# Step 0's attention over the nodes that a tile keeps, gathered by number, in a loop of small steps

## The chip, the cores and the metric

The kernel runs on one core of one Trainium2 chip. The metric is the time of one execution on the device in microseconds (us). Before the change three runs gave 1848.92, 1849.03 and 1849.40 us; the median is 1849.03. The profile was taken on an execution of its own, of 1845.05 us.

## What is computed

Two layers of a graph network on N = 3327 nodes with 256 features. Layer 0 is graph attention over a sparse adjacency (each row has a handful of neighbours) with a GRU cell and a layer norm; its result is X. Layer 1, which the change concerns, does two steps (n = 0 and 1):

```python
Xf = X
Xa = X
for n in range(STEPS):
    A = _top_p_attention(Xa, W1, W2, W3)
    Xf = R @ Xf
    Xa = A @ Xa
    Z = Z + Xf @ U1[n].T + Xa @ U2[n].T
```

`_top_p_attention` makes q = Xa W1ᵀ W2ᵀ, k = Xa W3ᵀ (64 wide), the logits q kᵀ and their softmax over all nodes. In each row it keeps the most probable nodes, as many as are needed to reach 0.9 of the sum, drops the others and divides by the sum of what is kept. R is the adjacency with the identity added, each row divided by its sum. The output is the layer norm of X + Z, added to X and normalized again.

## The kernel before

The rows are cut into NT = 26 tiles of 128 (the last has 127). Layer 0 (`Layer0.run`) runs its tiles in a software pipeline: `tile` (L835) is a generator whose pieces are numbered steps, a new tile starts every EVERY = 6 phases, and in each phase every open tile does one step, the oldest first. Within `manual_schedule` the instructions of the named engines keep the order in which the program writes them, PE, ACT, DVE and POOL in layer 0. At its end `Shared.qk` (L616) makes a tile's query and key: transposes, two products, copies into `qT` and `kT`. `first_logits` (L1009) already makes most logits of the first two tiles of step 0.

Layer 1 (`Layer1.run`, L1816) is one loop over 52 items, 26 tiles of step 0 and then 26 of step 1; PE, ACT and DVE keep the program's order there, POOL and the DMA queues of SP are ordered by the framework. An item goes through these pieces, spread over three turns of the loop:

- `chunk` (L1194): logits of the tile in eight pieces of 416 nodes, product on PE (L1201), copy out of PSUM on ACT (L1204);
- `list_1` (L1265): `eights` (L1217) takes the eight largest of every 208 nodes on DVE, `sort` (L1235, L1237) the 40 largest of those in order;
- `exp` (L1285) of all logits with the row's sum, `exp_list` of the 40 on ACT;
- `list_3` (L1304) with `settle` (L1240): running sum of the list, the least kept logit, and flags if the list was too short;
- `mask` (L1316): one DVE instruction over all 3327 nodes (L1325) sets what isn't kept to zero and sums the row;
- `product` (L1748): `turn` transposes the masked tile in 26 pieces on PE (L1408) and copies them on ACT (L1410, L1412), `times` (L1424) multiplies them with the 26 pieces of x1 (step 0) or xa (step 1);
- `scaled` (L1435) divides by the sum; in step 0 `rest` (L1742) then makes the next step's query and key, in four pieces between the products of the next item.

Beside it `fetch` (L1348) gathers the neighbours' rows with five indirect DMAs of POOL (L613) and makes five comparisons m on POOL (L1362); `propagate` (L1364) multiplies them (L1370). In step 0 POOL also makes `own` and x1 + bias (L1375 to L1380) and SP stores three arrays per tile.

```python
            slots = [[] for _ in range(7)]
...
                slot(5, self.mask, i + 1)
...
            self.product(i, slots)
```

The slots are the seven groups of `product`: what an item's product doesn't use of DVE and ACT is filled with the sorting, exp and mask of the next item and the logits of the next but one. Where step 0 ends (`new_step`) nothing can be filled in: the last tile's keys must exist before the logits of step 1 are complete.

If a flag in `bad` is set at the end, a slow version of the whole kernel runs after it; with these inputs it doesn't in the kernel before.

## Time and profile before

| what | value |
|---|---|
| profiled execution: its own time / span | 1845.05 / 1843.2 us |
| median of the runs | 1849.03 us |
| busy over the span: PE, DVE, ACT, POOL | 1642.9, 1317.1, 1022.7, 1157.2 us |
| last key copy of layer 0 ends | 390.3 us |
| first and last product of step 0 start | 407.3 and 973.8 us |
| first and last product of step 1 start | 998.9 and 1579.4 us |
| one round of step 0 (800.00 to 821.84): PE, DVE, ACT, POOL busy | 21.55, 12.74, 12.70, 14.20 us |
| mean granted TensorE clock | 0.962 of full |

In the profile a line gives engine, source line, operation, the tile written and those read, partitions x elements and count; then busy time, the mean duration of one and the idle time before it with what ended it. PE is TensorE's products, PEld its weight loads, DVE VectorE, ACT ScalarE, POOL GpSimd, SP the queue that issues most DMAs. In an answer by stretches each line has the stretch, its length, the busy time of each engine with its number of instructions, the granted TensorE clock, the busy share of the DMA engines and GB/s. In a timeline a line has start, duration, engine, line, operation and count, and in brackets the idle time before it.

### The profile page before, as it was taken

Reading aid. Unit: us, or ns where it says so; the run is one execution under the profiler, and the core shown is the slowest. Engines: PE = TensorE matmul, PEld = TensorE weight load, DVE = VectorE, ACT = ScalarE, POOL = GpSimd, SP = SyncE. Lnnn points to the kernel's source line nnn. Section 1 sums busy time; section 2 is a strip of 40 time slices with the busy share of each in tenths; the row PEclk is TensorE's granted clock in tenths of the full one; section 3 lists DMA queues with packets and bytes.
Section 4 is the critical chain, followed back from the end, with each engine's and each line's share of the span. In section 5 each row is a group of like instructions: output and inputs, shape, how many; then the busy total and the mean of one; then the engine's idle time right before and its main releaser. Section 6 shows DMA issues by size and latency. Waiting matters only on the chain. (4 is left out here: it accounts for less than half of the span.)

```text
span 1843.2 us, 27552 instructions
## 1 busy us (share of the span) xinstructions
PE 1642.9 (89%) x8093; PEld 1210.1 (66%) x8093; DVE 1317.1 (71%) x4100; ACT 1022.7 (55%) x2365; POOL 1157.2 (63%) x1902
## 2 busy tenths in 40 slices
PE   7488899969999999999996999999999989788992
PEld 5255555647777777777774777777777656677882
DVE  6788887455555665655546999999999877967751
ACT  3366666646565555555554555555555537558454
POOL 2577777557886666666655556566666583666654
PEclk9799999979999999999998999999999999899996
DMA  9876672222221111111101111111111120213321
GB/s 278 306 242 220 218 218 70 59 63 78 83 58 41 41 41 42 44 48 47 43 24 43 46 47 49 52 52 52 47 49 50 49 62 22 75 56 97 103 87 44
DMA packets 95098, 154.21 MB, mean 84 GB/s; under 512 B 16470, under 2 KB 68173, under 8 KB 94940
## 3 DMA queue, kind: packets, MB, share of 16 engines
q1 hardware_dynamic: 63818, 86.51, 14.4%
q0 software_dynamic: 20384, 53.28, 11.0%
q10 hardware_dynamic: 10738, 12.58, 2.1%
q8 instruction: 66, 1.08, 0.2%
q14 instruction: 92, 0.75, 0.1%
HBM read 124.65 MB, written 27.75 MB: 83 GB/s over the span
## 5 line engine op out<-in xcount | busy, mean ns | idle before, releaser
L1410 ACT COPY at<-pt 128x512 f32<-128x512 f32 (+2 forms) x364 | 191.6, 541 | 261.1 <-PE pt L1408 261.1
L1424 PE MATMUL pav<-xa,at 128*128 128x256 f32 (+2 forms) x1352 | 329.2, 388 | 7.3 <-ACT at L1410 7.3
L1424 PE MATMUL pav<-x,at 128*128 128x256 f32 (+2 forms) x1352 | 325.7, 385 | 7.6 <-ACT at L1410 7.6
L1424 PEld LDWEIGHTS pav<-xa,at 128*128 128x128 f32 (+2 forms) x1352 | 244.6, 190 | 86.5 <-ACT at L1410 41.0
L1424 PEld LDWEIGHTS pav<-x,at 128*128 128x128 f32 (+2 forms) x1352 | 244.4, 190 | 72.4 <-ACT at L1410 29.9
L1204 ACT COPY array<-pl 128x416 f32<-128x416 f32 (+4 forms) x405 | 183.1, 502 | 182.4 <-PE pl L1201 182.3
L1217 DVE MAX8 cand<-array 128x8 f32<-128x167 f32 (+5 forms) x921 | 239.0, 336 | 44.6 <-ACT array L1204 44.6
L613 POOL DMA_INDIRECT g<-xf_rows,edge x130 | 136.5, 1050 | 156.4 <-PE pxf L1370 124.1
L613 POOL DMA_INDIRECT g<-x_rows,edge x130 | 139.9, 1076 | 104.0 <-PE ptq L626 71.2
L1201 PE MATMUL pl<-kT,qT 64*128 64x416 f32 (+4 forms) x810 | 198.0, 560 | 4.5 <-ACT x L1599 2.7
L1309 DVE TENSOR_TENSOR_SCAN before<-e 128x40 f32<-128x40 f32 (+3 forms) x52 | 14.4, 276 | 224.2 <-ACT e L1302 224.2
L1362 POOL TENSOR_SCALAR m<-col,erow 128x128 f32<-128x128 f32 x260 | 162.8, 640 | 14.5 <-PE pxf L1370 8.0
L613 POOL DMA_INDIRECT g<-whx,edge x130 | 141.3, 1087 | 46.3 <-issue 36.1
L1370 PE MATMUL pxf<-g,m 128*128 128x256 f32 (+1 forms) x520 | 133.0, 404 | 14.7 <-POOL m L1362 8.0
L1370 PEld LDWEIGHTS pxf<-g,m 128*128 128x128 f32 (+1 forms) x520 | 98.6, 198 | 69.3 <-issue 41.9
L1235 DVE MAX8 lst<-cand 128x8 f32<-128x160 f32 (+3 forms) x364 | 114.5, 315 | 9.0
L1408 PE MATMUL pt<-ident,array 128*128 128x128 f32 (+1 forms) x676 | 100.9, 276 | 7.0 <-DVE array L1325 7.0
L819 DVE FIND_INDEX8 at<-ones,array 128x8 uint32<-128x840 f32 (+1 forms) x104 | 105.5, 1027 | 0.0
L1408 PE MATMUL pt<-ident,p 128*128 128x128 f32 (+2 forms) x676 | 99.6, 273 | 3.7 <-DVE p L1325 3.7
L1408 PEld LDWEIGHTS pt<-ident,array 128*128 128x128 f32 (+1 forms) x676 | 84.8, 144 | 24.8 <-PE pxf L1370 8.0
L1408 PEld LDWEIGHTS pt<-ident,p 128*128 128x128 f32 (+2 forms) x676 | 83.8, 143 | 20.8 <-PE pxf L1370 7.4
L1325 DVE SCALAR_TENSOR_TENSOR array<-array,t,array 128x3327 f32<-128x3327 f32 x26 | 96.0, 3692 | 0.5
(458 smaller groups left out, 3277.2 us busy)
## 6 DMA issues: line engine op xcount, KB each, us to landing
array<-in_adj_dram SPq DMA_DIRECT2D x23, 1248.0 KB, 6.7
array<-in_adj_dram SPq DMA_DIRECT2D x23, 415.5 KB, 6.4
xf_rows<-xf SPq DMA_DIRECT2D x50, 128.0 KB, 1.8
xa_rows<-xa SPq DMA_DIRECT2D x50, 128.0 KB, 1.7
xfs<-xf_rows SPq DMA_DIRECT2D x50, 128.0 KB, 2.4
whx<-table ACTq DMA_DIRECT2D x25, 129.5 KB, 3.9
x_rows<-x ACTq DMA_DIRECT2D x25, 128.0 KB, 1.7
xb_rows<-xb SPq DMA_DIRECT2D x25, 128.0 KB, 1.8
```

The source lines that it names most:

```text
L613: self.nc.gpsimd.indirect_dma_start(out=dst[:, b, :], out_offset=None, in_=table[:, :], in_offset=bass.IndirectOffsetOnAxis(ap=self.edge[: ...
L819: nc.vector.max_index(at[:r, g, :], self.ones8[:r], ad[:r, g, :])
L1201: nc.tensor.matmul(pl[:r, :w], q[on], self.sh.kT[on, n, s : s + w], start=True, stop=True)
L1204: nc.scalar.copy(l[:r, h * HALF + s : h * HALF + s + w], pl[:r, :w])
L1217: self.nc.vector.max(cand[:r, g * 8 : g * 8 + 8], src[:r, g * group : min(N, (g + 1) * group)])
L1235: nc.vector.max(lst[:r, k : k + 8], cand[:r])
L1325: nc.vector.scalar_tensor_tensor(v.p[:r], v.l[:r, :N], v.t[:r], v.p[:r], ALU.is_ge, ALU.mult, accum_out=sA[:r])
L1362: nc.gpsimd.tensor_scalar(v.m[:, b, :], sh.col1, sh.erow[:, v.at, b : b + 1], None, ALU.is_equal)
L1370: nc.tensor.matmul(acc[:r, :D], v.m[:, b, :r], v.g[:, b, :], start=(b == 0), stop=(b == EB - 1))
L1408: nc.tensor.transpose(pt[: rows(j), j - j0, :r], v.p[:r, cols(j)], self.ident[:r, :r])
L1410: nc.scalar.copy(at[:, :full, :r], pt[:, :full, :r])
L1424: nc.tensor.matmul(v.acc[: v.r, :D], at[:k, j - 4 * g, : v.r], V[:k, j, :], start=(j == 0), stop=(j == NT - 1))
```

## The change

Step 0 leaves the loop and gets one of its own, built like layer 0's: `sparse` is a generator of some 46 steps, a new tile starts every EVERY0 = 8 phases, and PE, ACT, DVE and POOL all keep the program's order. Logits, eights, sort and exp stay. The threshold becomes a limit half way between the least kept and the greatest dropped logit. Then nothing is masked or transposed: signs of logit minus limit (bf16) are made by ACT for the first 17 blocks of nodes and by DVE for the rest, PE counts over the rows which nodes any row of the tile keeps (`pc`), and these are numbered with a running sum (`pp`, `upto`, `at`). A place is split into a low part (32) and a high part (20); from both one-hot arrays are made (`hot`), and their product over all blocks gives the list of nodes by place (`pu`, `node`). The list goes through DRAM (`ulist`) to get one node per partition in five columns, and five indirect DMAs of POOL gather rows of `x1k`: features, a one and the key of step 0, 321 numbers. The logits of the gathered nodes are made once more, transposed (`plt`), with the limit subtracted by a product of ones and a diagonal; exp, and what is under 1 is set to zero. Five products with the gathered rows give the sum of features and, in the 257th column, the row's sum. More than 640 nodes in a tile set a flag in `bad`.

Layer 0's `qk` also makes the key by rows and stores the row of `x1k`, two DMAs on ACT's queue. The comparisons m of the propagation (L1362) are made by DVE in step 0, and the own row comes in by a product with the identity. x1 + bias moves to step 1 (`x_and_bias`), two tiles per item. `u1` is loaded after step 0, into the space of step 0's keys. The first two items' logits and the first one's eights of step 1 are made while the last tiles of step 0 run out (`first_1`). The loop over items now has step 1 alone.

```diff
...
+EVERY0 = 8
+UB = 5
+UL, UH = 32, UB * P // 32
+
+KX = D + 1 + DA
+
+ROUND = 1.5 * 2.0 ** 23
+
+SIGNS = (0, 8 * P, 17 * P)
...
+        if n == 0:
+
+            for c in range(DC):
+                nc.tensor.matmul(
+                    pq[:r, P : P + DA], xt[:, c, :r], self.wkqk[:, c, :DA], start=(c == 0), stop=(c == DC - 1)
+                )
...
+        if n == 0:
+            onek = self.onek[t % 2]
+            nc.scalar.copy(onek[:r, 1:], pq[:r, P : P + DA])
+            move_rows(nc.scalar, self.x1k[t * P : t * P + r, :D], src, r)
+            move_rows(nc.scalar, self.x1k[t * P : t * P + r, D:], onek[:r, :], r)
...
+    def sparse(self, t):
...
+        for k, pair in enumerate(self.chunks()):
+            yield from to(2 * k)
...
+                copies = [self.chunk(0, l, self.q(0, t), r, h, s, tag) for h, s in pair]
...
+            yield from to(2 * k + 1)
+            for copy in copies:
+                copy()
+            yield from to(2 * k + 2)
+            for h, s in pair:
+                c = h * HALF + s
...
+                    self.eights(v.cand, l, r, GROUP[0], c, min(N, c + LC))
+            if k < 3:
+                continue
+            v.last = self.last_eights(v.cand, r, tag)
+            sort = self.sort(v.cand, r, LIST[0], tag)
+            lst = next(sort)
+            nmax = small("nmax0", f"nmax{tag}")
+            nc.vector.tensor_scalar(nmax[:r], lst[:r, 0:1], -1.0, None, ALU.mult)
+        g1 = work.tile([P, EB, D], F32, tag="g", name=f"g{tag}")
+        sh.gather(g1, sh.x1_rows, t, (0, 1))
+        both = self.p[t % 2].bitcast(BF16)
+        signs, hot = both[:, : N + 1], both[:, N + 1 : N + 1 + NT * 2 * (UL + UH)].rearrange("p (b e) -> p b e", b=NT)
...
+        yield from to(9)
+        nc.scalar.activation(signs[:r, :HALF], l[:r, :HALF], AF.Exp, bias=nmax[:r], accum_out=sums[:r, 0:1])
+        next(sort)
+        next(sort)
+        sh.gather(g1, sh.x1_rows, t, (2,))
+        yield from to(10)
...
+        sh.gather(g1, sh.x1_rows, t, (3,))
+        yield from to(11)
+        nc.scalar.activation(e[:r, 1:], lst[:r, : LIST[0] - 1], AF.Exp, bias=nmax[:r])
+        sh.gather(g1, sh.x1_rows, t, (4,))
+        m1 = work.tile([P, EB, P], F32, tag="m", name=f"m{tag}")
+        for b in range(EB):
+            nc.vector.tensor_scalar(m1[:, b, :], sh.col1, sh.erow[:, t, b : b + 1], None, ALU.is_equal)
+        yield from to(12)
+        nc.scalar.activation(signs[:r, HALF:N], l[:r, HALF:N], AF.Exp, bias=nmax[:r], accum_out=sums[:r, 1:2])
+        yield from to(13)
...
+        nc.vector.tensor_tensor_scan(before[:r], e[:r], e[:r], 0.0, ALU.add, ALU.add)
...
+        nc.vector.tensor_scalar(thr2[:r], sums[:r, 0:1], sums[:r, 1:2], 2.0 * TOP_P, ALU.add, ALU.mult)
...
+        nc.vector.tensor_scalar(out[:r], before[:r], thr2[:r], BIG, ALU.is_ge, ALU.mult)
+        nc.vector.tensor_scalar(kept[:r], before[:r], thr2[:r], -BIG, ALU.is_lt, ALU.mult)
+        nc.vector.tensor_tensor(out[:r], out[:r], lst[:r], ALU.add)
+        nc.vector.tensor_tensor(kept[:r], kept[:r], lst[:r], ALU.add)
...
+        nc.vector.tensor_reduce(least[:r], out[:r], AX.X, ALU.min)
+        nc.vector.tensor_reduce(most[:r], kept[:r], AX.X, ALU.max)
+        nc.vector.tensor_scalar(most[:r], most[:r], v.last[:r], lst[:r, LIST[0] - 1 :], ALU.max, ALU.max)
+        nc.vector.tensor_scalar(self.flag[:r, 0, t : t + 1], most[:r], least[:r], None, ALU.is_ge)
+        nc.vector.tensor_scalar(most[:r], most[:r], least[:r], -0.5, ALU.add, ALU.mult)
+        nc.vector.tensor_scalar(least[:r], least[:r], -1.0, 1.0, ALU.mult, ALU.add)
...
+        nc.vector.tensor_tensor(limit[:r], most[:r], least[:r], ALU.min)
+        acc1 = self.pac.tile([P, 512], F32, tag="av", name=f"pxf{tag}")
+        nc.tensor.matmul(acc1[:r, :D], self.ident[:r, :r], sh.x1[:r, t, :], start=True, stop=False)
+        for b in range(EB):
+            nc.tensor.matmul(acc1[:r, :D], m1[:, b, :r], g1[:, b, :], start=False, stop=(b == EB - 1))
+        yield from to(14)
...
+        nc.scalar.activation(xf2[:r], acc1[:r, :D], AF.Copy, scale=sh.rinv[:r, t : t + 1])
+        move_rows(nc.sync, sh.xf_rows[t * P : t * P + r, :], xf2[:r], r)
...
+        nc.vector.memset(signs[:, N:], 0.0)
+        nc.scalar.activation(signs[:r, s0:s1], l[:r, s0:s1], AF.Sign, bias=limit[:r])
+        yield from to(15)
+        nc.scalar.activation(signs[:r, s1:s2], l[:r, s1:s2], AF.Sign, bias=limit[:r])
...
+        nc.vector.tensor_scalar(bound[:r], limit[:r], -1.0, None, ALU.mult)
+        nc.vector.tensor_scalar(signs[:r, s2:N], l[:r, s2:N], bound[:r], None, ALU.is_ge)
+        yield from to(17)
+        pc = self.psm.tile([P, 512], F32, tag="sm", name=f"pc{tag}")
+        for b in range(NT):
+            nc.tensor.matmul(
+                pc[:, b : b + 1], signs[:r, b * P : (b + 1) * P], self.ones16[:r, 0:1], start=True, stop=True
+            )
+        yield from to(18)
...
+        nc.vector.tensor_scalar(any_[:, :full], pc[:, :full], 0.5 - r, None, ALU.is_gt)
+        nc.vector.tensor_scalar(any_[:, full:], pc[:, full:NT], 0.5, None, ALU.is_gt)
+        yield from to(19)
+        pp = self.psm.tile([P, 512], F32, tag="sm", name=f"pp{tag}")
+        nc.tensor.matmul(pp[:, :NT], sh.lower16, any_, start=True, stop=True)
+        nc.tensor.matmul(pp[:, NT : 2 * NT], self.ones16, any_, start=True, stop=True)
+        yield from to(20)
...
+        nc.vector.tensor_tensor_scan(upto, pp[:, NT : 2 * NT], self.zeros, 0.0, ALU.add, ALU.add)
+        nc.gpsimd.tensor_copy(self.needed[:, t : t + 1], upto[:, NT - 1 :])
...
+        nc.vector.tensor_tensor(at, upto, pp[:, NT : 2 * NT], ALU.subtract)
+        nc.vector.tensor_tensor(at, at, pp[:, :NT], ALU.add)
...
+        whole = upto
+        nc.vector.tensor_scalar(whole, at, 1.0 / UL, (1.0 - UL) / (2.0 * UL), ALU.mult, ALU.add)
+        nc.vector.tensor_scalar(whole, whole, ROUND, None, ALU.add)
+        nc.vector.tensor_scalar(whole, whole, -ROUND, None, ALU.add)
+        nc.vector.scalar_tensor_tensor(low, whole, -float(UL), at, ALU.mult, ALU.add)
+        nc.vector.scalar_tensor_tensor(high, any_, -128.0, whole, ALU.mult, ALU.add)
...
+        nc.vector.tensor_tensor(hot[:, :, e0:e1], wide(low, UL), deep(self.places_l, UL), ALU.is_equal)
+        yield from to(21)
+        nc.vector.tensor_tensor(hot[:, :, e1:e2], wide(high, UH), deep(self.places_h, UH), ALU.is_equal)
+        nc.vector.tensor_scalar(hot[:, :, :e0], hot[:, :, e0:e1], self.fromend, None, ALU.mult)
+        nc.vector.tensor_tensor(hot[:, :, e2:e3], hot[:, :, e1:e2], wide(self.block, UH), ALU.mult)
+        yield from to(22)
+        pl = self.psm.tile([P, 512], F32, tag="sm", name=f"pu{tag}")
+        for b in range(NT):
+            nc.tensor.matmul(
+                pl[:e1, : 2 * UH], hot[:, b, :e1], hot[:, b, e1:e3], start=(b == 0), stop=(b == NT - 1)
+            )
+        yield from to(23)
...
+        nc.scalar.activation(node, pl[UL:e1, UH : 2 * UH], AF.Copy, scale=float(P))
+        yield from to(24)
+        nc.vector.tensor_tensor(node, node, pl[:UL, :UH], ALU.add)
+        nc.sync.dma_start(self.ulist[t].rearrange("(l h) -> l h", h=UH), node)
...
+        nc.sync.dma_start(back, self.ulist[t].rearrange("(p b) -> p b", b=UB))
+        yield from to(27)
...
+        nc.gpsimd.tensor_scalar(idx, back, -1.0, float(N + 1), ALU.mult, ALU.add)
...
+        def gather(b):
+            nc.gpsimd.indirect_dma_start(
+                out=g2[:, b, :], out_offset=None, in_=sh.x1k[:, :],
+                in_offset=bass.IndirectOffsetOnAxis(ap=idx[:, b : b + 1], axis=0),
...
+            )
+        gather(0)
+        yield from to(28)
+        gather(1)
+        gather(2)
+        yield from to(29)
+        gather(3)
+        yield from to(30)
+        gather(4)
+        yield from to(33)
+        pt = self.ptr.tile([P, 512], F32, tag="tr", name=f"pk{tag}")
+        for b in range(UB):
+            k, on = g2[:, b, D + 1 :], slice(b // 2 * P, (b // 2 + 1) * P)
+            if b % 2:
+                nc.tensor.matmul(pt[DA:, on], k, self.ident, start=True, stop=True)
+            else:
+                nc.tensor.transpose(pt[:DA, on], k, self.ident)
...
+        nc.scalar.activation(diag[:r, :r], self.ident[:r, :r], AF.Copy, scale=limit[:r])
+        yield from to(34)
...
+        nc.scalar.copy(kg[:, : UB // 2, :], pt[:, : UB // 2 * P].rearrange("p (j c) -> p j c", c=P))
+        nc.scalar.copy(kg[:DA, UB // 2, :], pt[:DA, UB // 2 * P : (UB // 2 + 1) * P])
+        yield from to(35)
+        pls = [self.ptr.tile([P, 4, P], F32, tag="tr", name=f"plt{tag}_{k}") for k in range(2)]
+        for k, n in enumerate(((UB + 1) // 2, UB // 2)):
+            nc.tensor.matmul(
+                pls[k][:, :n, :r], sh.ones[:r, :], diag[:r, :r].unsqueeze(1).to_broadcast([r, n, r]),
+                start=True, stop=False,
+            )
+        for b in range(UB):
+            on = slice(b % 2 * DA, (b % 2 + 1) * DA)
+            nc.tensor.matmul(
+                pls[b % 2][:, b // 2, :r], kg[on, b // 2, :], self.q(0, t)[on], start=False, stop=(b + 2 >= UB)
+            )
+        yield from to(37)
...
+        for k, n in enumerate(((UB + 1) // 2, UB // 2)):
+            nc.scalar.activation(w[:, k::2, :r], pls[k][:, :n, :r], AF.Exp)
+        yield from to(38)
+        nc.vector.scalar_tensor_tensor(w[:, :, :r], w[:, :, :r], 1.0, w[:, :, :r], ALU.is_ge, ALU.mult)
+        yield from to(39)
+        acc = self.pac.tile([P, 512], F32, tag="av", name=f"pav{tag}")
+        for b in range(UB):
+            nc.tensor.matmul(acc[:r, : D + 1], w[:, b, :r], g2[:, b, : D + 1], start=(b == 0), stop=(b == UB - 1))
+        yield from to(40)
...
+        nc.vector.tensor_scalar(rA[:r], acc[:r, D : D + 1], 1e-30, None, ALU.max)
+        nc.vector.reciprocal(rA[:r], rA[:r])
+        yield from to(42)
+        xa = self.xa[:r, t, :]
+        nc.scalar.activation(xa, acc[:r, :D], AF.Copy, scale=rA[:r])
+        move_rows(nc.sync, sh.xa_rows[t * P : t * P + r, :], xa, r)
+        yield from to(43)
+        yield from sh.qk(self.psm, self.work, 1, t, xa)
+    def step_0(self):
+        tiles, first = [], self.first_1()
+        self.done = self.phase = 0
+        while self.phase < EVERY0 * NT or tiles:
+            if self.phase % EVERY0 == 0 and self.phase // EVERY0 < NT:
+                tiles.append(self.sparse(self.phase // EVERY0))
+            for g in list(tiles):
+                if next(g, True):
+                    tiles.remove(g)
+                    self.done += 1
+            next(first, None)
+            self.phase += 1
...
...
+    def first_1(self):
...
+        while self.phase < EVERY0 * NT + 8:
+            yield
...
+        self.fetch(NT)
...
+        for pair in self.chunks():
+            while self.done * P < min(NT * P, HALF + pair[0][1] + LC):
+                yield
+            for i in (NT, NT + 1):
+                self.some_logits(i, pair)
+                yield
...
+    def x_and_bias(self, t):
+
+        nc, sh, r = self.nc, self.sh, rows(t)
+        xb = self.work.tile([P, D], F32, tag="own", name=f"xb{t}", bufs=2)
+        nc.gpsimd.tensor_tensor(xb[:r], sh.x1[:r, t, :], self.b[:r], ALU.add)
+        move_rows(nc.sync, sh.xb_rows[t * P : t * P + r, :], xb[:r], r)
...
+        engines = {mybir.EngineType.PE, mybir.EngineType.Activation, mybir.EngineType.DVE}
+        with self.tc.manual_schedule(engines=engines | {mybir.EngineType.Pool}):
+            self.step_0()
+        with self.tc.manual_schedule(engines=engines):
+            self.list_1(NT)
...
+            self.load_u1()
+            for i in range(NT, total):
...
+                for t in range(2 * (i - NT), 2 * (i - NT) + 2):
+                    if t < NT:
+                        self.x_and_bias(t)
...
```

## The prediction

> **What bounds the kernel now.** I read the busy shares of the page first, then the busy time by stretches, which cuts the span into stages: layer 0 up to about 390 us, step 0 from 407 to 974, step 1 from 999 to 1580, the ends after that.
>
> ```profile
> core 0: us, PE busy (x) PEld busy (x) DVE busy (x) ACT busy (x) POOL busy (x), PEclk, DMA share, GB/s
> 390.00:407.30 17.30, 7.44 (x22) 5.39 (x22) 13.90 (x50) 5.55 (x12) 13.76 (x13) 0.52 0.25 65
> 407.30:974.00 566.70, 557.01 (x2832) 420.60 (x2832) 319.04 (x1073) 323.34 (x688) 387.80 (x451) 1.00 0.17 50
> 974.00:998.90 24.90, 9.37 (x37) 6.46 (x36) 17.99 (x52) 8.03 (x17) 7.47 (x14) 0.69 0.08 19
> 998.90:1579.60 580.70, 550.10 (x2749) 410.29 (x2748) 527.68 (x1613) 315.81 (x612) 351.23 (x596) 0.99 0.18 49
> ```
>
> The reader is to see: in step 0 PE works 557 of 566.7 us, 26 rounds of 21.84 us, one tile each; DVE and ACT have over 40% to spare. So step 0 is bound by PE, with the 26 transposes (L1408) and 26 products (L1424) of a tile. Step 1 is bound by PE and DVE together and isn't rewritten.
>
> Three timelines give the prices that the page's means don't: what an instruction costs inside a queue.
>
> ```profile
> 244.69 0.17 PE L889 MATMUL pe<-tell,mem 128*128 128x20 bf16 x1
> 244.72 0.17 PE L890 MATMUL pe<-tell,mem 128*128 128x19 bf16 x1
> ...
> 825.93 1.99 PE L1424 MATMUL pav<-x,at 128*128 128x256 f32 x8 [0.29 <-ACT at L1410]
> ```
>
> Small bf16 products start 0.025 us apart although each shows 0.17; fp32 ones of 256 columns are two instructions of about 0.217 each.
>
> ```profile
> 837.21 0.24 DVE L1247 TENSOR_SCALAR out<-before,pay 128x40 f32<-128x40 f32 x1
> 837.49 0.20 DVE L1249 SCALAR_TENSOR_TENSOR kept<-out,lst 128x40 f32<-128x40 f32 x1
> ...
> 838.31 3.67 DVE L1325 SCALAR_TENSOR_TENSOR array<-array,t,array 128x3327 f32<-128x3327 f32 x1
> ```
>
> Small DVE instructions that wait for each other stand 0.16 to 0.3 us apart; the mask over all nodes (L1325) is one of 3.67.
>
> ```profile
> 829.52 1.00 POOL L613 DMA_INDIRECT g<-x_rows,edge  x1 [0.30 <-issue]
> 838.48 3.60 POOL L1261 TENSOR_SCALAR many<-d 128x1 f32<-128x1 f32 x1
> ```
>
> A gather occupies POOL for 1.30 us with its gap. The 3.60 us of L1261, on one element per row, are POOL held by DVE's mask.
>
> **What the Trainium skill says.** "SBUF — State Buffer", section "SBUF: two separate sides": DVE and GpSimd share a port pair under an exclusive lock. The trace agrees for POOL (the 3.60 us); it shows no DVE instruction stretched by gathers: the mask of layer 0 (L884) took 535 to 599 ns in all 26 calls while POOL gathered almost without pause. "VectorE: DVE Perf Modes", section "Mode 2×_1P": a two-tensor instruction gets two results a cycle only with 16-bit data at step 1; the new comparisons read one operand at step 0, so I take one element a cycle. L900 (80 elements, 0.243 us) gives the fixed part, about 0.16. "TensorE: Matmul & The Clock Gate", section "Part 1: The HAM clock gate": TensorE falls to half clock after an idle window of some 3.4 us. The trace agrees in kind: 1.00 where PE is full, 0.52 and 0.69 where it is mostly idle.
>
> **The change, part by part.** Worked out in float64 from the reference's inputs, a row of step 0 keeps 1 to 32 nodes and the 128 rows of a tile together 369 to 513. So 640 places suffice everywhere, and the slow path isn't taken for that.
>
> PE, per tile. Gone: 26 transposes × 0.14 = 3.6 and 52 × 0.217 = 11.3. Kept: logits 16 × 0.175 = 2.8, propagation 2.2, query and key 0.8. Added: one identity product 0.4, counts and list 54 bf16 products × 0.025 and their latency 1.7, five key turns 0.9, logits by node 1.75, five products 2.2. Sum 12.8: PE is no longer the bound.
>
> ACT: the copies at/pt (L1410) go, two Signs come (1664 elements took 1.69, so 1.05 and 1.2), with small ones: 14.2.
>
> POOL: ten gathers × 1.30, two small ones: 13.7; the five comparisons m, own, xb, and the held flags leave it.
>
> DVE, per tile: MAX8 16 × 0.281 = 4.5; sorting 3.2 (both as in the timeline of before); five comparisons m at 0.2 from L561's 0.268 = 1.0; threshold 13 small × 0.21 = 2.7; Sign's DVE share 1151 elements: L884 took 0.54 for 640, so 0.8, with bound and memset 1.0; any 0.3; numbering 8 small = 1.85; one-hot: 832 elements / 0.96 + 0.16 less overlap 0.95, 520 elements twice 0.62, one scalar multiply 0.3, sum 2.5; node 0.2; weights 640 elements 0.8; reciprocal 0.4; the rest 0.25. Sum 18.7 against 12.74 now. One-hot at two elements a cycle would make it 17.7; every small one at 0.25 instead makes it 19.7. So **DVE is the new bound**, with 18.7 against today's 21.84.
>
> Waits that stay. Tiles start every eight phases and each engine's order is fixed, so I laid one round out by hand. Two waits don't fit. First, the numbering's prefix product pp stands on PE behind the logits by node, which wait for ACT's key copy kg, itself behind Exp 1.69, two copies 0.88 and two small 0.9 after nmax; PE then needs 1.9, so pp is ready 5.55 us after nmax, and DVE arrives after 4.98 (sort 2.5, any, MAX8, m): 0.6 us, with DVE's whole queue behind it. Second, rA waits for the five products, 2.5 us after the weights, where DVE has 2.1 of other work: 0.45. PE will be about 65% busy; the first 100 us (59%) show a clock of 0.86, the ends (76%) 0.90, the stretch 360 to 407 (66%, with single waits of over 3 us) 0.78. I take 0.88, which lengthens the 3.95 us of PE in these two chains by 0.55. Round: 18.7 + 0.6 + 0.45 + 0.55 = 20.3.
>
> The list's way through DRAM: store landing 1.8, load 2.0 (xf_rows and xf in the page's DMA issues); three phases, about 6 us, lie between: hidden. The new wait is POOL's: `uidx` waits for the list, and behind it stand this tile's five gathers and one of a younger tile; POOL has 6 us of slack a round. If that cover went, the 4 us would fall there, then on PE's key turns. On SP, behind `back`, wait only xa's and xf's stores, not needed soon.
>
> Step 0 as a whole, from the last key copy at 390 to the first product of step 1. Before: 998.9 − 390 = 609 us. After: five opening rounds, by the DVE work of the one to five tiles present (the first is a wait for the last logits): 3 + 13 + 17.5 + 17.8 + 19 = 70; 21 full rounds × 20.3 = 426; one round without new MAX8 17; then the last tile alone: list 9, DRAM 4.5, POOL (which first serves step 1's fetch, 9.5, and the tile before) until 25.4, landing 2, keys to key copy 12.3, logits and MAX8 of step 1's first tile 3.3, its sort, exp and mask 17.2 as now (979.9 to 997.1): 60. Sum 573. Gain 36.
>
> Layer 0: two more products per tile (four instructions × 0.13 = 0.5 us on PE), one copy and two DMA issues on ACT (0.9 us). POOL sets the pace there: it never waits, a round is 11.37 us, ACT waits 2.75 for its `shift` each round, PE is idle about 1.25. Both are covered until the last five tiles, where PE runs without gaps: 5 × 0.5; at the end 1.6 of ACT's issues stand before the first logits. I take 5; without the cover 13 to 23; a gain is excluded, since only work is added.
>
> Step 1: xb's addition (0.73 on POOL) and store move there, two per tile for 13 tiles; POOL is 60% busy, SP far less: 1, at worst 4 through the shared port. The load of u1 moves off the start, unread until the ends: 0.
>
> Sum: −36 + 5 + 1 = −30 on the profiled execution: span 1843.2, so 1813; its own time of 1845.05 becomes 1815. The median of the runs is 1849.03, 4 us above that execution, so **1819**.
>
> **Rivals.**
> (a) The waits close: if the chain to pp beats DVE by its missing 0.6, the reciprocal finds its products ready and the clock stays full, a round is 18.7 and the step saves 34 more: 1785. For: layer 0, built the same way, keeps its bound engine full. Against: my layout of the order.
> (b) Slower, by TensorE's clock. PE's gaps in a round reach 2 to 3 us; if they count as idle, the 3.95 us of PE in the two chains stretch: at 0.6 by 2.63 instead of 0.55, 21 × 2.1 + 4 = 48 us more: 1867. It decides from a clock of about 0.68 down, where the stretch is 1.8 a round in place of 0.55 and eats the 30 us. For: 0.69 at 974 to 999. Against: 0.86 to 0.90 in the stages nearest in load.
> (c) POOL becomes the bound: DVE's two-input and fast-mode instructions fill some 9 us of a round, and each of ten gathers may be held. From 0.8 us a gather POOL passes 21.7; at 1.0 a round is 23.7: 1890. Against: in layer 0, beside a DVE 85% busy, gathers took 1.09 on average against 1.00.
> (d) Layer 0 pays in full and the numbering costs 0.6 more: everything is given back, 1849.
>
> **How the numbers follow.** Forecast 0.45 (its own range 1800 to 1840), (a) 0.25, (b) 0.15, (c) 0.08, (d) 0.07. Below 0.2% (3.7 us) a measurement here can't tell from no change. Faster 0.45 + 0.25 = 0.70; same 0.06 of (d); slower the rest, 0.24. The range leaves out 0.08 below 1775 (rounds under 18.2) and 0.12 above 1868 (most of (c), half of (b)).
>
> **What would show it.** In the changed profile: step 0's DVE near 92% busy and PE near 65%; 26 tiles' xa in rounds of 20.3; DVE waiting 0.5 to 1.2 us for PE at the numbering (pp) and at rA, and for little else; POOL's gathers near 1.0 to 1.1; PEclk 0.85 to 0.9; layer 0's last x_rows store within 5 us of today's; step 1's rounds unchanged at 22.3. I am wrong if DVE waits in more places than these two, if the small instructions stand further apart than 0.21, or if step 1 moves.

## The result, and the profile after

The changed kernel takes 1958.47 us (median of 4 runs, 1954.40 to 1963.17; the kernel before beside it 1848.97). The ratio is 1.0595 with a 95% interval of 1.0569 to 1.0622: slower by 6%, where 1819 was forecast. The profiled execution has a span of 1957.8 us against 1843.2, so 114.6 us are to be found.

The stages of the changed kernel, as busy time by stretches (columns as before: stretch, length, busy time of PE, PEld, DVE, ACT and POOL, granted clock, DMA share, GB/s): twenty rounds of step 0, step 1's first twelve items, its other fourteen.

```profile
478.40:919.40 441.00, 358.98 (x2381) 231.54 (x2381) 333.08 (x1421) 255.65 (x541) 223.98 (x241) 0.88 0.31 80
...
1034.80:1371.50 336.70, 277.44 (x1265) 203.60 (x1264) 249.50 (x761) 139.47 (x275) 208.22 (x296) 0.90 0.16 47
1371.50:1693.30 321.80, 298.94 (x1483) 223.18 (x1484) 282.69 (x853) 176.13 (x338) 195.54 (x321) 0.98 0.17 48
```

The reader is to see two things. In step 0 no engine is full: DVE works 333 of 441 us (76%), PE 359 (81%); a round takes 22.05. So DVE isn't the bound that was forecast; waits are. And step 1, whose code is hardly touched, is slow in its first part: in the 336.7 us of twelve items, eleven take 27.7 to 30.6 each, where an item before took 21.8; afterwards it is back at 21.8 until the items that were longer before the change too.

Between the landmarks of the stages (the start of layer 0's last key copy, step 1's first product, its last product, the end) the time moved like this:

| us | before | after | difference |
|---|---|---|---|
| layer 0, to its last key copy | 390.0 | 399.2 | +9.2 |
| step 0, from there to step 1's first product | 608.9 | 635.6 | +26.7 |
| step 1, to its last product | 580.6 | 658.5 | +77.9 |
| ends | 263.7 | 264.5 | +0.8 |

The waits of the changed kernel, longest first, of which these lines matter (engine, instruction and line, what it waited for: us in total, times, longest us):

```profile
DVE upto L1355 <- PE pp L1352: 77.4, 24, 4.2
PE pos L1823 <- POOL flag L1821: 73.0, 13, 9.2
...
DVE rA L1451 <- PE pav L1448: 43.2, 26, 5.2
...
POOL own L1687 <- DMA xb_rows<-xb: 23.0, 11, 3.2
```

The second and the last belong to step 1. The other two are the two waits that the prediction had named; in the twenty rounds of step 0 they are 65.5 and 23.5 us, 4.45 a round, where 1.6 was forecast.

**Step 1, one slow item.** POOL's timeline (start, duration, engine, line, operation, in brackets the idle time and its cause) of the changed kernel, after it DVE's two long instructions over all nodes, then PE's:

```profile
1159.24 0.72 POOL L1695 TENSOR_TENSOR xb<-x,ln_b 128x256 f32<-128x256 f32 x1 [1.70 <-DMA xb_rows<-xb]
1163.13 0.93 POOL L1687 TENSOR_SCALAR own<-xf,rinv 128x256 f32<-128x256 f32 x1 [3.17 <-DMA xb_rows<-xb]
1164.05 0.29 POOL L1578 TENSOR_SCALAR lim<-last,lst 128x1 f32<-128x1 f32 x1
1164.50 4.50 POOL L1853 DMA_INDIRECT left_over<-pay,idx  x1 [0.17 <-DVE array L1654]
...
1170.38 0.19 POOL L1821 CAST flag<-flag 128x1 bf16<-128x1 f32 x1
```

```profile
1160.71 3.62 DVE L1654 MATCH_REPLACE8 array<-gone,array 128x3335 f32<-128x3335 f32 x1
1164.36 3.68 DVE L1640 SCALAR_TENSOR_TENSOR p<-array,t,p 128x3327 f32<-128x3327 f32 x1
```

```profile
1170.62 0.16 PE L1823 MATMUL pos<-flag,lower 128*128 128x1 bf16 x1 [6.28 <-POOL flag L1821]
```

It reads as a chain. `xb` and `own` have the same tag and so take turns in two buffers. An `xb` buffer is free only when its store has landed; POOL stands still 1.70 and then 3.17 us. In that time DVE gets to the second of its long instructions, the mask L1640, and POOL's scatter L1853, which takes 1.09 us elsewhere, takes 4.50 and ends 0.96 us after the mask. `flag` comes that much later, and on PE the small product `pos` waits 6.28 us for it, with the next item's logits and transposes behind it.

Which POOL instruction meets the mask changes from item to item. The one above is the only slow item in which it is the scatter; an item with usual values is this (POOL, then DVE):

```profile
1103.93 0.93 POOL L1687 TENSOR_SCALAR own<-xf,rinv 128x256 f32<-128x256 f32 x1 [1.85 <-DMA xb_rows<-xb]
...
1105.30 1.09 POOL L1853 DMA_INDIRECT left_over<-pay,idx  x1 [0.17 <-issue]
1106.45 3.80 POOL L1580 TENSOR_SCALAR short<-lim,t 128x1 f32<-128x1 f32 x1
```

```profile
1102.82 3.62 DVE L1654 MATCH_REPLACE8 array<-gone,array 128x3335 f32<-128x3335 f32 x1
1106.47 3.69 DVE L1640 SCALAR_TENSOR_TENSOR p<-array,t,p 128x3327 f32<-128x3327 f32 x1
```

The scatter beside the first long instruction takes its 1.09; L1580, which takes 0.3 elsewhere, takes 3.80 and ends 0.09 us after the mask. In all eleven slow items one POOL instruction is held in this way, for 2.7 to 4.5 us. Before the change the mask began 2.7 to 3.1 us after POOL had made `flag`, so nothing of this chain met it.

**Step 0, one round.** The changed kernel's PE timeline, then its DVE timeline, then the granted clock by stretches, cut where the clock changes (columns: stretch, length, PE busy, clock, DMA share, GB/s):

```profile
699.84 2.12 PE L1430 MATMUL plt<-diag,ones 128*128 128x384 f32 x4
701.89 0.93 PE L1436 MATMUL plt<-qT,kg 64*128 64x128 f32 x10
702.75 0.19 PE L1351 MATMUL pp<-any,lower 128*128 128x26 bf16 x1
```

```profile
695.04 0.14 DVE L1272 TENSOR_SCALAR nmax<-lst 128x1 f32<-128x1 f32 x1
...
703.00 0.21 DVE L1355 TENSOR_TENSOR_SCAN upto<-pp,zeros 128x26 f32<-128x26 f32 x1 [3.27 <-PE pp L1352]
...
717.37 0.16 DVE L1451 TENSOR_SCALAR rA<-pav 128x1 f32<-128x1 f32 x1 [2.71 <-PE pav L1448]
```

```profile
694.77:698.18 3.41, 2.01 (x33) 1.00 0.03 3
698.18:701.60 3.42, 3.42 (x9) 0.50 0.16 46
701.60:705.01 3.41, 3.41 (x25) 1.00 0.49 130
```

PE is busy 2.01 of 3.41 us, and the next 3.41 us run at half clock, just where a younger tile's logits and the first of the logits by node (plt) stand, with `pp` behind them. The mean of 0.88 over the step, which was forecast, is made of stretches at 1.00 and of stretches at 0.50: in the 441 us of the twenty rounds 26 of these last 3.41 us and two 6.83, 102 us in all. In most rounds one lies in the chain to `pp` that DVE waits for. In every second or third round the five products pav fall into such a stretch as well; the wait at rA is then 2 to 2.7 us instead of 0.49.

### The profile page after: what moved, and what is told of

It is laid out like the page before. It is cut to its first block, busy times and chain, and to the rows that moved or that the text cites. A ratio compares the mean times of both kernels' runs of the same rounds, so it can differ in the third digit from the quotient of the medians.

```text
span 1957.8 us, 28975 instructions
## 1 busy us (share of the span) xinstructions
PE 1598.3 (82%) x8425; PEld 1121.8 (57%) x8425; DVE 1423.8 (73%) x4835; ACT 1030.7 (53%) x2388; POOL 1119.1 (57%) x1800
## 5 line engine op out<-in xcount | busy, mean ns | idle before, releaser
L1525 ACT COPY array<-pl 128x416 f32<-128x416 f32 (+3 forms) x402 | 182.2, 504 | 188.2 <-PE pl L1522 187.6
L1522 PE MATMUL pl<-kT,qT 64*128 64x416 f32 (+3 forms) x804 | 238.5, 621 | 45.9 <-ACT array L1525 42.0
L1397 POOL DMA_INDIRECT g<-x1k,uidx x130 | 138.9, 1068 | 52.1 <-issue 36.7
L1725 ACT COPY at<-pt 128x512 f32<-128x512 f32 (+2 forms) x182 | 96.0, 542 | 134.1 <-PE pt L1723 134.0
L1522 PEld LDWEIGHTS pl<-kT,qT 64*128 64x128 f32 (+1 forms) x804 | 80.7, 201 | 89.9 <-ACT array L1525 51.6
L1448 PE MATMUL pav<-g,w 128*128 128x257 f32 (+1 forms) x260 | 85.1, 490 | 33.7 <-DVE w L1444 31.6
L1393 POOL TENSOR_SCALAR uidx<-back 128x5 uint32<-128x5 f32 x26 | 5.1, 195 | 156.9 <-DMA back<-ulist 156.8
L1654 DVE MATCH_REPLACE8 array<-gone,array 128x3335 f32<-128x3335 f32 (+1 forms) x26 | 94.0, 3616 | 0.0
L1558 DVE MATCH_REPLACE8 cand<-lst,cand 128x160 f32<-128x160 f32 (+3 forms) x312 | 92.9, 298 | 0.0
L1674 POOL TENSOR_SCALAR m<-col,erow 128x128 f32<-128x128 f32 x130 | 76.5, 601 | 1.1
L969 PE MATMUL acc<-g,m 128*128 128x259 f32 (+1 forms) x260 | 64.8, 397 | 6.8 <-ACT m L965 6.8
```

The source lines that it names most:

```text
L1397: nc.gpsimd.indirect_dma_start(out=g2[:, b, :], out_offset=None, in_=sh.x1k[:, :], in_offset=bass.IndirectOffsetOnAxis(ap=idx[:, b : b + 1 ...
L1448: nc.tensor.matmul(acc[:r, : D + 1], w[:, b, :r], g2[:, b, : D + 1], start=(b == 0), stop=(b == UB - 1))
L1522: nc.tensor.matmul(pl[:r, :w], q[on], self.sh.kT[on, n, s : s + w], start=True, stop=True)
L1525: nc.scalar.copy(l[:r, h * HALF + s : h * HALF + s + w], pl[:r, :w])
L1654: nc.vector.match_replace(rev, gone[:r], rev, -BIG)
L1725: nc.scalar.copy(at[:, :full, :r], pt[:, :full, :r])
```

## The experiments

All times are beside runs of the kernel before on the same chip; the ratio is to these. "Item" is one tile of step 1, "round" one tile of step 0 (mean of the first twenty).

### Step 1: buffers or work

`e1_own_apart`:

```diff
-        xb = self.work.tile([P, D], F32, tag="own", name=f"xb{t}", bufs=2)
+        xb = self.work.tile([P, D], F32, tag="hx", name=f"xb{t}")
```

> The changed kernel, with xb of x_and_bias in the two buffers of tag hx (idle in step 1 at that time) in place of the two that it shares with own; the same additions and stores stay in the same first 13 items of step 1. Theory (a wait on buffers): xb and own take turns in two buffers, each waits for a store to land, POOL comes some 5 us late to lim and the scatter, these fall into the long mask of DVE, and PE's product pos waits 6 us for flag. Then the first 13 items go back from 28.9 us to 22 to 23 and the whole from 1958 to 1870 to 1890. Rival (the work itself: two additions on POOL and two more stores on SP an item): items stay above 26, the whole above 1925.

Measured: 1888.64 us, 1.0215 (1.0189 to 1.0241), 70 us less than the changed kernel. From the second item on an item takes 21.3 to 21.9. The run has a flaw: the framework orders POOL in step 1, and with free buffers it put 15 of the 26 additions ahead of step 1 and the other eleven into the first item, which took 35.7 us. So work and waits had left the slow items together. `e6_adds_only` keeps the work in place:

```diff
         gather(4)
+        self.x_and_bias(t)
         yield from to(33)
...
-                        self.x_and_bias(t)
+                        self.x_and_bias(t, False)
...
-        move_rows(nc.sync, sh.xb_rows[t * P : t * P + r, :], xb[:r], r)
+        if store:
+            move_rows(nc.sync, sh.xb_rows[t * P : t * P + r, :], xb[:r], r)
```

> The changed kernel, with xb made and stored in step 0 (one tile each, after the last gather of the list), while step 1's first 13 items keep their two additions at the same places of POOL's queue and in the same two buffers with own, but store nothing. Theory (the wait for a store to land before own may be written): without stores the buffers are free at once, the items go from 28.9 to 21.8 to 22.6 us, the whole to 1870 to 1890. Rival (two additions on POOL, 1.5 us an item, make it late enough to fall into DVE's mask): items stay above 26, the whole above 1925.

Measured: 1904.74 us, 1.0315 (1.0293 to 1.0336); the items take 21.6 to 22.0. POOL's timeline of this kernel has both additions at their old place, right ahead of `own`:

```profile
1174.03 1.54 POOL L1696 TENSOR_TENSOR xb<-x,ln_b 128x256 f32<-128x256 f32 x2
1175.67 1.02 POOL L1688 TENSOR_SCALAR own<-xf,rinv 128x256 f32<-128x256 f32 x1
...
1177.28 1.09 POOL L1855 DMA_INDIRECT left_over<-pay,idx  x1
...
1179.73 0.19 POOL L1823 CAST flag<-flag 128x1 bf16<-128x1 f32 x1
```

No idle time stands in brackets, the scatter takes 1.09 again, `flag` is ready and PE's wait for it went from 73.0 us in 13 places to 17.1 in 2. So the two additions cost almost nothing: from the first to the last propagation (ACT's instruction `xf`) step 1 takes 573.8 us here, 649.0 in the changed kernel and 570.8 before. What costs is the store. This kernel drops the two stores of an item together with the wait for them, so it doesn't part the two by itself; that it is the wait is read from the timelines above, in which POOL stands still until the landing (42.1 us in 22 places of step 1). The whole came down by only 54 since step 0, which now makes and stores `xb`, became 19 us longer (rounds of 22.77); the forecast of 1870 to 1890 missed that.

### Step 0: the place of pp, POOL's copy, the clock

`e3_needed_dve`:

```diff
-        nc.gpsimd.tensor_copy(self.needed[:, t : t + 1], upto[:, NT - 1 :])
+        nc.vector.tensor_copy(self.needed[:, t : t + 1], upto[:, NT - 1 :])
```

> The changed kernel, with the copy to needed on DVE instead of POOL, so that the rounding of the numbering (which overwrites upto) no longer waits for POOL's queue of gathers. Theory: only the 7.4 us of such waits in 6 rounds and part of the 9.8 us at the last tile come back, and DVE gets 26 copies of 0.1 to 0.15: the whole falls by 5 to 15 us, to 1943 to 1953. Rival (the waits for pp and pav take it up, as they end later than DVE in any case): no change, within 3 us of 1958.

Measured: 1944.44 us, 1.0507 (1.0473 to 1.0542), as the theory has it. The gain is at the end of the step, not in the rounds (21.89). DVE writes the rounding over `upto`, and so waits for POOL to have copied its last column (7.4 us in 6 places of the changed kernel). At the last tile it is the reading of all of `needed` (L2202), ahead of the rounding, that waits for the same copy: POOL first serves two fetches of step 1 and three gathers of the list:

```profile
975.17 0.18 DVE L2202 TENSOR_REDUCE bad<-needed 128x1 f32<-128x26 f32 x1 [9.82 <-POOL needed L1356]
```

`e4_pp_first`:

```diff
-        yield from to(19)
         pp = self.psm.tile([P, 512], F32, tag="sm", name=f"pp{tag}")
```

> The changed kernel, with the two prefix products pp issued one small step earlier, so that on PE they stand ahead of the logits by node (plt) of an older tile instead of behind them. Theory (DVE is held by the place of pp in PE's queue): the 3.25 us that DVE waits for pp each round vanish; the older tile's chain (plt, w, pav, rA) then arrives later relative to DVE and takes back about 1; rounds fall from 22.05 to about 19.5, the whole to 1885 to 1910. Rival (the chain kg, plt, w, pav sets the round and pp only shows it): the wait moves to w or rA, rounds stay above 21.3, the whole above 1940.

Measured: 1928.45 us, 1.0409 (1.0356 to 1.0462), rounds of 21.00: between the two expectations. The wait for `pp` is gone, and another has come in its place (DVE's waits from 480 to 900 us):

```profile
DVE upto L1362 <- POOL needed L1355: 48.6, 20, 4.3
DVE rA L1450 <- PE pav L1447: 27.6, 20, 2.7
```

DVE now arrives 3 us earlier and meets the copy of the last experiment, behind POOL's gathers: 2.4 us a round. The wait for `pp` had hidden it.

`e5_pe_filled` leaves the order and fills PE's gaps (and so adds work that nobody reads):

```diff
+    def busy(self, ps, n):
+        for _ in range(n):
+            self.nc.tensor.matmul(ps[:, 384:512], self.ident, self.ident, start=True, stop=True)
...
+        self.busy(pc, 8)
...
+        self.busy(pl, 8)
...
+        self.busy(acc, 5)
```

> The changed kernel, with fp32 products of identity by identity that nobody reads put into PE's three gaps of a step-0 round: 8 after the counts pc, 8 ahead of the list's products pu, 5 ahead of the five products pav. Theory (TensorE's clock halves after each gap, and just the chain kg to pp and pav then runs at half speed): the granted clock of step 0 rises from 0.88 to 0.97 or more, pav's ten instructions take 2.4 us instead of 4.65 in every round, DVE waits about 1.5 instead of 3.25 for pp, and rounds fall from 22.05 to 19.5 to 20.5, the whole to 1905 to 1930. Rival (the order alone holds DVE, the clock only follows from it): rounds stay at 21.5 to 22.5, or grow by the 21 products, the whole 1945 to 1975.

Measured: 1929.54 us, 1.0428 (1.0396 to 1.0460), rounds of 20.49, clock from 500 to 900 us 0.99 against 0.88. Groups of PE in step 0's rounds (busy us, mean ns of one), first the changed kernel, then this one:

```profile
L1448 PE MATMUL pav<-g,w 128*128 128x257 f32 x200 | 62.4, 472 | 24.2 <-DVE w L1444 24.2
...
L1430 PE MATMUL plt<-diag,ones 128*128 128x384 f32 (+1 forms) x80 | 43.9, 699 | 0.0
```

```profile
L1456 PE MATMUL pav<-g,w 128*128 128x257 f32 x200 | 47.3, 383 | 0.0
...
L1437 PE MATMUL plt<-diag,ones 128*128 128x384 f32 (+1 forms) x84 | 26.1, 433 | 0.0
```

PE does 21 products more in a round, and the round is 1.56 us shorter. DVE's wait for `pp` fell from 3.25 to 0.26 us a round (5.4 us in 21 rounds), but not all of this is the clock. Two lines of one round:

```profile
558.66 0.14 DVE L1277 TENSOR_SCALAR nmax<-lst 128x1 f32<-128x1 f32 x1
...
565.00 0.21 DVE L1361 TENSOR_TENSOR_SCAN upto<-pp,zeros 128x26 f32<-128x26 f32 x1
```

From the end of `nmax` to the use of `pp` it is 6.2 us here and 7.8 in the round shown before: the clock gives 1.6. The rest of the fall is DVE itself, which comes to this point 1.6 us later, because it waits elsewhere: 1.26 us a round for the eight products that stand in the counts' own tile, ahead of `any`, and after `pp` another 0.81 for POOL's copy. So the half clock in the chain is shown to be a cause, of about half of the wait, and filling shown to be a poor cure.

### The repairs together

`e7_three_mended` has the edits of e3 and e4, and `xb` made and stored in step 0 instead of step 1.

> The changed kernel with three edits together: xb made and stored in step 0, the copy to needed on DVE, the prefix products pp one small step earlier. Theory: the first products alone turned 3.25 us of waiting for pp into 2.5 for POOL's needed, and the copy alone left the wait for pp; together both go, and DVE's own 17.5 us a round with 0.5 to 2.2 for pav remain: rounds of 18 to 19.7, step 1 as before the change, the whole 1785 to 1825. Rival (the chain kg, plt, w, pav at half clock takes their place): rounds above 20.5, the whole above 1835.

Measured: 1824.29 us, 0.9884 (0.9866 to 0.9903): 1.2% faster than before the change. Rounds of 19.45, items of 21.8. In its profile layer 0 ends at 397.0 (+7), step 0 up to the first propagation of step 1 takes 564.9 us against 604.4 before (−39.5), step 1 573.3 against 570.8. What is left of DVE's waits (480 to 880 us):

```profile
DVE thr L1303 <- ACT p L1297: 13.5, 9, 2.3
DVE thr L1303 <- ACT array L1297: 13.2, 10, 2.2
DVE rA L1451 <- PE pav L1448: 10.3, 21, 0.5
```

`thr` waits for ACT's second Exp, which stands on ACT behind the copies of query and key and so behind PE.

`e9_stores_sp` (the three repairs, and the two stores of x1k in layer 0 issued by `nc.sync` instead of `nc.scalar`):

> The same three edits, and layer 0's two stores a tile of x1k issued by SP in place of ACT. Theory: layer 0's last key copy, which came 6 to 9 us later than before the change (390.0), is late by ACT's issues: it comes at 391 to 394, the whole falls by 3 to 6. Rival (PE's two more products and the copy cost it): it stays at 396 or later and the time within 3 us.

Measured: 1817.79 us, 0.9834 (0.9808 to 0.9859), but layer 0's last key copy at 397.4, where the kernel without the edit had 397.0. In two later kernels with the same edit it was at 392.9 and 391.6; in all fifteen profiles with ACT's stores between 395.7 and 399.2. This speaks for ACT's issues as part of layer 0's loss, and e9 against. The median is 6.5 us under e7's, but the profiled executions, which are compared here, don't show it (1822.34 us, in e7 1814.59); so it stays unsettled, at 4 to 6 us.

### Beyond the repairs: fills and moves that don't add up

`e8_filled` puts 8 products into the second logits chunk's tile, 8 ahead of pu, 5 ahead of pav; `e10_filled_ahead` 4 ahead of pp, 4 of pu, 3 of pav. Both stand on the three repairs.

> The same three edits, and PE's gaps filled with products that nobody reads: 8 ahead of one logits chunk after the counts, 8 ahead of pu, 5 ahead of pav. Theory of the clock: pav always takes 2.4 us, the wait for it falls to 0.5 or less, rounds come to 17.6 to 18.3, 10 to 30 us below the same edits without filling. Rival (with DVE no longer held, PE's gaps are short and the clock no longer matters): within 8 us of it, or slower by the products' own time.

> The three mended edits, and PE's gaps filled with products that nobody reads in tiles that are free ahead of the wait: 4 ahead of pp, 4 ahead of pu, 3 ahead of pav (in the last filled kernel 8 of them stood behind a wait for ACT and cost 2 us a round themselves). Theory of the clock: without the half clock after the counts pq comes about 2 us earlier, so ACT's second Exp and DVE's thr2, which now waits 1.3 to 2.2, come without a wait; rounds from 19.5 to 17.9 to 18.5, the whole to 1780 to 1800. Rival (the fills' own time and the order eat it): rounds of 19.2 or more, the whole above 1815.

Measured: 1892.28 us, 1.0225 (1.0191 to 1.0260) and 1875.79 us, 1.0158 (1.0101 to 1.0214); rounds of 22.55 and 21.36. The clock rose to 0.95 and 0.96, and the rounds grew. In e8 the fills had to wait 0.5 us for ACT to free their tile and then ran 2.0 us ahead of the real product; `pq` and pav came later by that, and rA's wait rose to 3.0 us a round. In e10 the wait at rA doubled (30.2 us from 480 to 900, in e7 14.1); which of its fills did it wasn't separated. With the order mended, both sets of fills cost more than the clock gave back.

`e11_exp_early` moves the second Exp one small step earlier (`yield from to(12)` left out), `e12_exp_ra` moves rA from step 40 to 41 as well, `e13_all` adds 3, 4 and 3 fills.

> The three mended edits, and ACT's second Exp one small step earlier, ahead of the copies of the younger tile's logits and of qT and kT, for which ACT waits 2.85 us on PE. Theory (thr2's wait comes from that order on ACT): DVE's wait at thr2 goes, 17.5 us of DVE and 0.5 for pav remain, rounds of 18.0 to 18.8, the whole 1785 to 1805. Rival (the logits' copies come 1.7 later and PE and DVE wait for these): rounds of 19.2 or more, the whole above 1815.

> As the kernel with the early Exp, and the reciprocal rA one small step later on DVE. Theory: the 0.5 us for pav goes as well, DVE's own 17.5 sets the round, the whole 8 to 14 below the early Exp alone. Rival (xa, query and key come later and hold ACT): the same within 5 or slower.

> As the kernel with early Exp and late rA, and 3, 4 and 3 products that nobody reads ahead of pp, pu and pav. Theory: with both moves DVE no longer waits for the chain on PE, and the clock matters little: within 8 us of the kernel without them. Rival (the half clock still holds something back): 10 or more us faster.

Measured: 1865.75 us, 1.0078 (1.0047 to 1.0108); 1868.19 us, 1.0106 (1.0064 to 1.0147); 1963.45 us, 1.0605 (1.0529 to 1.0680). Rounds of 21.36, 21.31 and 25.68. Every theory failed; the rivals of e11 and e12 have the right range, but not the reason of what follows. The wait at `thr` did go, but a new one came. DVE's and then POOL's timeline of e11:

```profile
796.09 0.28 DVE L1557 MATCH_REPLACE8 cand<-lst,cand 128x128 f32<-128x128 f32 x1
801.19 0.18 DVE L1346 TENSOR_SCALAR any<-pc 128x17 bf16<-128x17 f32 x1 [4.83 <-remote]
```

```profile
796.77 1.00 POOL L631 DMA_INDIRECT g<-x_rows,edge  x1 [0.30 <-issue]
798.07 1.00 POOL L1395 DMA_INDIRECT g<-x1k,uidx  x1 [0.30 <-issue]
799.37 1.00 POOL L1395 DMA_INDIRECT g<-x1k,uidx  x1 [0.30 <-issue]
800.67 1.00 POOL L1395 DMA_INDIRECT g<-x1k,uidx  x1 [0.31 <-issue]
```

The counts pc, which `any` needs, end at 798.07 by the profile, and `any` starts 3.1 us later. Such waits of 1.4 to 5.0 us were in 6 rounds of e11, 11 to 12 of e12 and 15 to 16 of e13, each within a run of POOL's gathers, 0.3 us apart, that went on while pc ran and when `any` was due; in e7 POOL was not gathering when `any` was due, in every full round, and no such round waits. In e11 these waits are 20.5 us, about half of what its twenty rounds lost against e7 (38 us); the rest is longer waits at rA and for ACT's copies of the logits, as the rival had it, and longer DVE instructions. Three kernels asked why. `e14_any_two_inputs` is e11 with

```diff
-        nc.vector.tensor_scalar(any_[:, :full], pc[:, :full], 0.5 - r, None, ALU.is_gt)
-        nc.vector.tensor_scalar(any_[:, full:], pc[:, full:NT], 0.5, None, ALU.is_gt)
+        nc.vector.scalar_tensor_tensor(any_[:, :full], pc[:, :full], r - 0.5, self.zeros[:, :full], ALU.add, ALU.is_gt)
+        nc.vector.scalar_tensor_tensor(any_[:, full:], pc[:, full:NT], -0.5, self.zeros[:, full:], ALU.add, ALU.is_gt)
```

`e15_counts_early` is e11 and `e16_counts_three` is e7, with pc at step 16 instead of 17.

> The kernel with three repairs and the early Exp, and any made by scalar_tensor_tensor (pc plus a constant, compared with a tile of zeros) in place of tensor_scalar with one input. Theory A (DVE's one-input instruction waits for the port that it shares with POOL, whose gathers hold it): the waits of 1.4 to 4.9 us at any go, rounds fall from 21.4 to 18.2 to 19, the whole to 1780 to 1805. Theory B (the counts pc on PE finish late while a gather runs, whatever DVE does): the waits stay, rounds of 21 to 21.8, the whole 1855 to 1880.

> The kernel with three repairs and the early Exp, and the 26 counts pc one small step earlier, ahead of the key turns pk on PE, so 1.5 to 2 us earlier and ahead of the first gather of the list in most rounds. Theory B (pc beside a gather finishes late): the waits at any become rare, rounds of 18.2 to 19.3, the whole 1780 to 1815. Theory A (DVE's any beside a gather waits): any stands where it stood, the waits stay, the whole above 1850.

> The kernel with the three repairs alone, and the counts one small step earlier. There, no round waits at any; so both theories expect the rounds at 19.2 to 19.8 and the whole within 10 us of 1824. Rival (the turns pk, now between the counts and pp, keep PE busier and the clock full): rounds below 18.8.

Measured: 1812.53 us, 0.9836 (0.9804 to 0.9868); 1810.81 us, 0.9812 (0.9796 to 0.9829); 1810.10 us, 0.9815 (0.9793 to 0.9837). Rounds of 19.24, 19.19 and 19.26: e14 a little above what theory A expected, e15 within theory B's range, e16 within both for the rounds, and 14 us below e7 where at most 10 were expected. Both cures work, each as its own theory has it and against the other, and so they don't tell the theories apart: with the wait gone, POOL's gathers fall elsewhere too, and in no full round of e14 or e15 is one running when `any` is due.

The traces of e11, e12 and e13 do tell them apart. They record when the one semaphore changes that `any` waits for, with which PE reports the end of pc. In the rounds of e7, e14, e15 and e16 it changes 0.01 to 0.02 us after pc's end by the profile. In the late rounds of e11 it changes 1.6 to 3.2 us after it, in those of e13 up to 3.75, and `any` starts 0.02 us after the change each time; the word `remote` in the line above stands for this, a change at which no recorded instruction ends. So DVE doesn't hold `any` back: PE's report of the counts is late, as theory B has it, and that e14 also cured it comes from where its gathers fell. Two early rounds agree that the one-input form isn't to blame: in e7 at 449.18 and in e12 at 476.77 it started without delay inside a gather. Why a run of gathers delays PE's report, and why some gathers beside pc don't, stays open.

`e17_together` has e11's early Exp, e14's and e15's edits and e9's stores on the three repairs, `e18_together_ra` also rA at step 41.

> The kernel with three repairs, early Exp, early counts, any made by the form with two inputs and layer 0's stores on SP. Theory (DVE's sum is the floor, the parts overlap): rounds of 18.8 to 19.3, the whole 1800 to 1813. Rival (each gives its part): rounds of 18 to 18.5, the whole 1780 to 1795.

> The same, and rA one small step later on DVE. Theory: the 0.7 us a round that DVE waits for pav go, rounds of 18.0 to 18.7, the whole 10 to 18 us below the kernel without it. Rival (xa, query and key come later and PE waits instead): within 5 us or slower.

Measured: 1841.83 us, 0.9965 (0.9944 to 0.9987), and 1819.89 us, 0.9846 (0.9822 to 0.9869). Together they are worse than apart: in e17 rounds of 20.38 with 2 us of waiting at rA in most; in e18 (rounds of 19.55) that wait is gone and DVE waits 1.6 us a round for ACT's copies of the logits instead (35.0 us in 29 places from 480 to 900). Neither expectation of e17 was met, and of e18's only that it would be faster than e17. Rounds of 19.2 are as far as these runs came; the fastest versions are e14, e15 and e16, which their intervals don't part, 1.6 to 1.9% below the kernel before.

## Why the prediction was wrong, point by point

Forecast and measurement in the profiled execution differ by 145 us (1813 against 1957.8): step 1 by 76.9, step 0 by 62.6, layer 0 by 4.2, the ends by 0.8.

- **Step 1, "xb's addition (0.73 on POOL) and store move there ... POOL is 60% busy, SP far less: 1, at worst 4".** This step failed worst, and by its method. It priced the work (0.73 us, measured 0.72) by a busy share and didn't ask which buffers the moved instructions use and who frees them. Measured: +77.9. The two waits for a landing (mostly 1.7 and 1.85 us an item), a POOL instruction held beside the mask (2.7 to 4.5 us instead of 0.2 to 1.1) and the in-order `pos` on PE made 5 to 9 us an item of it; e6 shows that the additions alone cost almost nothing. The worst case of 4 looked at the shared port alone, without the delay that brings POOL into the mask. The sentence "wrong if step 1 moves" was the right sign to look for.
- **"So DVE is the new bound, with 18.7".** Too high: DVE is busy 16.6 us a round, and without its listed waits a round would be 17.45. The list of prices was sound; small instructions overlap a little more than was taken (the thirteen of the threshold stand 0.19 us apart in the round shown, not 0.21). PE's sum of 12.8 was too low, which cost nothing in this sum: PE is busy 17.9 us a round, 81% instead of 65%, of which 0.88 of the clock explains 1.7.
- **Two waits, "0.6 us ... and 0.45", and "0.88, which lengthens ... by 0.55".** The places were right, pp and rA, the sizes wrong: 3.25 and 0.49 or 2.15 where 1.6 in all was forecast. Three terms of the wait at pp failed. The largest is the clock. 0.88 was the measured mean exactly, but the clock isn't 0.88 anywhere: the Trainium skill, "TensorE: Matmul & The Clock Gate", "Part 1: The HAM clock gate", says that the gate passes either half or all of the pulses, and the stretches above agree (0.50, then 1.00). A mean over a step must not be put on a chain in which a half-clock stretch lies; it lengthens this one by 1.6 us (7.8 against 6.2 in e5), where 0.55 was taken for both chains. The prediction also took from that section that an idle window of some 3.4 us is needed. Here no gap of PE in the twenty rounds was longer than 2.4 us; half clock followed stretches of 3.41 us in which PE was busy 1.6 to 2.3. The second term is the order: PE still has a younger tile's logits and query to do when `kg` is ready, so even with the full clock of e5 pp comes 6.2 us after nmax, not 5.55. The third is DVE, which arrives 4.6 us after nmax, not 4.98.
- **Round 20.3.** Measured 22.05; 21 rounds make 37 of step 0's 62.6. The other 26 are in the opening and the drain: there 173 us are spent instead of 147, 9.82 of them at `needed`.
- **`needed`** was counted among POOL's "two small ones" and its effect on DVE costed at nothing. The prediction didn't see that DVE overwrites its source. Alone it is worth 14 us (e3), and 2.4 us a round as soon as pp doesn't hide it (e4).
- **Layer 0, "I take 5".** 9.2 in this profile, 5.7 to 9.2 in all fifteen with the same code. The term was too small; which part of the added work it is stays open (e9).
- **POOL's wait for the list, "hidden".** Right: uidx waits 156.8 us in 25 places in the changed kernel, and PE's key turns don't wait for it.
- **The rivals.** (b), the clock, named the right mechanism and the point at 0.68, but compared it with a mean of 0.86 to 0.90; it gave 1867 and could not see step 1. (c) didn't come: in the twenty rounds the gathers took 1.07 and 1.10 us on average, against 1.00 alone. (d) named the numbering and layer 0, but at 0.6 us more a round where it was 2.65 more, and at 13 to 23 us where layer 0 lost 9.2. None had a moved step that stalls on its buffers, and the range, to 1868, took its width from the rewritten stage alone.

What the forecast took for the change's worth was nearly there: with three small repairs (e7) the median is 1824.29 against the forecast 1819, and step 0 gives 39.5 us where 36 were forecast. That the profiled span, 1812.5, meets the forecast 1813 is luck: it is of the fastest of five runs, and its rounds are shorter than forecast (19.45, not 20.3) while the opening and drain are longer.

## What to carry to other kernels

When a step is moved, list the buffers that it writes, who frees each (a store frees it only when it has landed), and which in-order product far away waits for the last small instruction behind it. Look where the half-clock stretches lie, put half the clock, not the mean, on a TensorE chain that begins in one, and look whether another engine's whole queue stands behind that chain. A copy handed to an idle engine is no gift when its source is overwritten next: the owner then waits for that engine's queue.

## What the runs showed of the hardware

- Beside DVE's fp32 SCALAR_TENSOR_TENSOR over 3327 elements (3.7 us) a POOL instruction lasted until this had ended: 2.7 to 3.8 us for small ones that take 0.2 to 0.3 elsewhere, 4.50 for the scatter by indirect DMA. Beside the fp32 MATCH_REPLACE8 over 3335 elements (3.6 us) nothing was held: the scatter took 1.09 there in seven items, as it does alone. The Trainium skill, "SBUF — State Buffer", "SBUF: two separate sides", says that a DVE instruction with two SBUF inputs, or in a 2-port mode, and a GpSimd instruction that reads SBUF lock each other out of a shared pair of ports for a whole instruction. The trace agrees: SCALAR_TENSOR_TENSOR here reads two SBUF arrays of 3327 elements a row, MATCH_REPLACE8 only one (and eight values).
- In step 0 the clock was half for 26 stretches of 3.41 us and two of 6.83 (102 us in all, of 441). They came after stretches of 3.41 us in which PE was busy for 1.6 to 2.3 us; no gap of PE was longer than 2.4 us, and PE was busy 81% on average.
- Beside a run of POOL's gathers PE reported the end of 26 small products up to 3.75 us late (e11, e12, e13; above). The cause is open.
